# Two x tiles of a key stage: loaded together, one chain of statistics, normalised and turned two products later

## The chip, the cores and the metric

The kernel runs on one core of a Trainium2 chip. The metric is the device time of one execution in microseconds (us), the median of several runs. The core's engines each work through a queue of their own in order: TensorE (PE in the profile, its weight loads PEld) multiplies, VectorE (DVE) and ScalarE (ACT) work on tiles, GpSimd (POOL) does small arithmetic and issues some DMAs, SyncE (SP) issues most DMAs. An instruction that waits holds up all that stands behind it in the same queue.

## The reference

16 batches of 64 tokens with 512 features go through one block: cross attention with 32 heads of 128, and a linear layer with eight low-rank experts.

```
x = x + xattn(layernorm(x), ctx, mask, bias, Wq, Wk, Wv, Wo)
x = x + ffn(layernorm(x), base_W, base_b, router, A, B, expert_map)

xattn: q = xn @ Wq ; k = ctx @ Wk ; v = ctx @ Wv      # (1024 x 512) @ (512 x 4096)
       score = q k^T / sqrt(128) + bias, masked ; p = softmax(score)
       out = (p v) @ Wo
layernorm(x) = (x - mean) / sqrt(var + 1e-5)           # over the 512 features
```

All is float32. The change touches only the first layernorm, and when it is done.

## The kernel before

**Tiles and stages.** The 1024 tokens of x are eight tiles of 128 tokens. Keys and values are computed first, then queries, attention and output projection head pair by head pair, then the linear layer. A float32 product is three matmuls (`mm3`, line 256): both factors are split into a high and a low part (`split`, line 69: a cast on ACT, "gh" in the profile, and a subtraction on DVE, "gl").

**A stage.** The keys come in eight quarters of four heads, the values in stages of eight heads. Each stage is one 2 x 2 block product made with seven block products instead of eight (`winograd`, line 213). The products run in the order 1, 2, 6, 5, 7, 4, 3 (`ORDER`). In a key stage a product has two halves k (two PSUM banks), each of six matmuls. Products 1, 6, 7 and 4 add up in the same bank xb[k]; after products 1, 6 and 7 a copy of the sum so far is taken on ACT (u, u2, u3; lines 220, 227, 230), and the next product of that bank must wait for the copy. Products 5 and 3 add up in yb[k]. The results c11, c22, c21 and c12 are made by DVE and ACT into eight buffers ("ob") and stored by SP (`emit_k`, line 338).

**The order of the stages.** `stages` (line 381) lists them: quarters 0 and 1 run interleaved, then value stage, 2, 3, value stage, 4, 5, value stage, 6, value stage, 7. So quarter 5 follows quarter 4 directly. While a stage runs, the weights of the next are split.

**The x tiles.** Quarters 3 to 6 each handle two tiles of x beside their products (`keys_of`, line 366). A tile is loaded by SP (`x_tile`, line 315, xt), normalised (`norm`, line 87) and turned (`x_turn`, line 325). `norm` does, on DVE, the statistics and the aggregate (lines 92, 93) and adds 1e-5 (line 95), on POOL the power -0.5 (line 96, "rs"), on DVE the shift (line 98, "nb"), and on ACT the normalising (line 100, "xn"). `x_turn` transposes 32 x 32 blocks on DVE (line 330, "xb") and then issues 16 DMAs of 16 KB from POOL's queue, which move the blocks to their places in xT (line 333). xt, xn, xb, and later the v tiles of the attention, share four buffers (pool "v"). xT is first read after quarter 6.

**What sets the order.** The order on TensorE is written out. On DVE, ACT, POOL and SP a planner orders the instructions by the priority in which the program names them and by its own estimate of when they become ready; `tc.issue_after(ins)` adds that an instruction is queued behind `ins`. The normalising is queued behind the last copy taken so far (`copied[-1]`), the load of x behind the last store of keys (`stored[-1]`).

Of the kernel before, what the change touches and what calls it, by code (L numbers as in the profile page):

```python
# [14 lines left out]
AF = mybir.ActivationFunctionType  # L15
# [32 lines left out]
def xattn_ffn_kernel(ctx: ExitStack, tc: tile.TileContext, x, ctxT, wq, wk, wv, wo, fside, mask,  # L48
                     base_wT, base_b, arT, router_b, lora_b, expert_map, out):
    nc = tc.nc  # L50
    scale = 1.0 / math.sqrt(128.0)

    small = ctx.enter_context(tc.tile_pool(name="small", bufs=1))
    sm = ctx.enter_context(tc.tile_pool(name="sm", bufs=2))
# [11 lines left out]
    def blk(tag, name, dt=F32, shape=(P, 512)):  # L66
        return pools[tag].tile(list(shape), dt, tag=tag, name=name)
# [16 lines left out]
    nc.vector.memset(zero, 0.0)  # L84
    maskb = const.tile([P, NT, S], F32, name="maskb")

    def norm(pool, xns, xts):
        n = len(xts)
        mv = pool.tile([P, n, 2], F32, tag="mv", name="mv")
        for j, xt in enumerate(xts):  # L90
            bs = pool.tile([P, 6], F32, tag="bs", name="bs")
            nc.vector.bn_stats(bs, xt)
            nc.vector.bn_aggr(mv[:, j, :], bs)
        rs = pool.tile([P, n], F32, tag="rs", name="rs")
        nc.vector.tensor_scalar(rs, mv[:, :, 1], EPS, None, ALU.add)
        nc.gpsimd.tensor_tensor(rs, rs, nhalf[:, 0:n], ALU.pow)
        nb = pool.tile([P, n], F32, tag="nb", name="nb")
        nc.vector.scalar_tensor_tensor(nb, mv[:, :, 0], -1.0, rs, ALU.mult, ALU.mult)
        for j, (xn, xt) in enumerate(zip(xns, xts)):
            nc.scalar.activation(xn, xt, AF.Identity, bias=nb[:, j:j + 1], scale=rs[:, j:j + 1])  # L100

    def transposed(ps, xn):
        for kc in range(KC):
# [5 lines left out]
    with ExitStack() as actx:  # L109
# [103 lines left out]
        def winograd(mm, n, emit, yzbank=bank, order=ORDER):  # L213

            xb, zb, yb, u, u2, u3 = ({} for _ in range(6))

            def post(i, k):
                if i == 1:
                    u[k] = blk("sn", "u")
                    nc.scalar.copy(u[k], xb[k])  # L220
                elif i == 2:
                    c = blk("ob", "c11")
                    nc.vector.tensor_tensor(c, u[k], zb[k], ALU.add)
                    emit(0, 0, k, c)
                elif i == 6:
                    u2[k] = blk("sn", "u2")
                    copied[:] = [nc.scalar.copy(u2[k], xb[k])]
                elif i == 7:
                    u3[k] = blk("sn", "u3")
                    copied[:] = [nc.scalar.copy(u3[k], xb[k])]  # L230
                    c = blk("ob", "c22")
                    nc.vector.tensor_tensor(c, u3[k], yb[k], ALU.add)
                    emit(1, 1, k, c)
                elif i == 4:
                    c = blk("ob", "c21")
                    nc.scalar.copy(c, xb[k])
                    emit(1, 0, k, c)
                elif i == 3:
                    c = blk("ob", "c12")
                    nc.vector.tensor_tensor(c, u2[k], yb[k], ALU.add)  # L240
                    emit(0, 1, k, c)

            for i in order:
                for k in range(n):
                    if i == 1:
                        xb[k] = bank()
                    elif i == 2:
                        zb[k] = yzbank(k)
                    elif i == 5:
                        yb[k] = yzbank(k)  # L250
                    b = xb if i in (1, 6, 7, 4) else zb if i == 2 else yb
                    mm(i, k, b[k], i in (1, 2, 5))
                    post(i, k)
                yield i
# [7 lines left out]
        def mm_weights(t, g):  # L262
            def mm(i, k, o, first):
                for kc in range(2):
                    mm3(o, [a[:, kc, k * P:(k + 1) * P] for a in g[i]], [b[:, kc] for b in t[i]],
                        first and kc == 0, kc == 1)
            return mm
# [47 lines left out]
        def x_tile(t):  # L315
            nonlocal xT
            if xT is None:
                xT = ax.tile([P, KC, TOK], F32, tag="ax", name="xT")
            xt = blk("v", "xt")
            with tc.issue_after(stored[-1].ins):  # L320
                nc.sync.dma_start(out=xt, in_=x[t])
            xn = blk("v", "xn")
            return xn, xt

        def x_turn(t, xn):

            a, g = divmod(t, 4)
            dst = xT.rearrange("p k (g a b) -> p g a k b", g=4, a=2)[:, g, a]
            xb = blk("v", "xb", F32, (P, 4, KC, 32))
            nc.vector.transpose(xb, xn.rearrange("p (k j i) -> p j k i", k=KC, j=4))  # L330
            for j in range(4):
                for i in range(4):
                    nc.gpsimd.dma_start(out=dst[32 * j:32 * j + 32, :, 32 * i:32 * i + 32],  # L333
                                        in_=xb[32 * i:32 * i + 32, j])
# [3 lines left out]
        def emit_k(q):  # L338
            def emit(i, j, k, c):
                stored[:] = [nc.sync.dma_start(out=kd[4 * q + 2 * i + k][:, j * HALF:(j + 1) * HALF], in_=c)]  # L340
            return emit
# [8 lines left out]
        with tc.manual_schedule(engines={nc.tensor.engine}):  # L350
# [13 lines left out]
                    enumerate((bank, lambda k: small_bank("yz")))]  # L364

            def keys_of(q, g):
                xn = {}
                for i in winograd(mm_weights(tc_, g), 2, emit_k(q)):
                    if 3 <= q < 7:
                        t = 2 * (q - 3)  # L370
                        if i in (1, 6):
                            xn[i] = x_tile(t + (i == 6))
                        if i in (6, 7):
                            with tc.issue_after(copied[-1].ins):
                                norm(sm, *([a] for a in xn[1 if i == 6 else 6]))
                        elif i == 5:
                            x_turn(t, xn[1][0])
                        elif i == 3:
                            x_turn(t + 1, xn[6][0])

            stages = (0, "o"), (2, "k"), (3, "k"), (2, "o"), (4, "k"), (5, "k"), (4, "o"), (6, "k"), (6, "o"), (7, "k")
            ops = {}
# [17 lines left out]
            for n, (q, kind) in enumerate(stages[:-1]):  # L400
                load(n + 2)
                ops[n + 1].all()
                if kind == "k":
                    keys_of(q, ops[n])
                else:
                    for i in winograd(mm_oct(tc_, ops[n]), 4, emit_oct(q),
                                      lambda k: bank() if k < 2 else small_bank("yz")):
                        pass
                if n == 1:
                    with tc.issue_after(stored[-1].ins):  # L410
                        nc.sync.dma_start(out=m8, in_=mask)
                        nc.sync.dma_start(out=emi, in_=expert_map.partition_broadcast(P))
                        nc.sync.dma_start(out=rb, in_=router_b.partition_broadcast(P))
                    nc.vector.tensor_scalar(maskb, m8, -1.0, BIG, ALU.add, ALU.mult)
                    nc.vector.tensor_reduce(valid, m8, AX.X, ALU.max)
                    nc.vector.tensor_copy(emf, emi)
                    for e in range(E):
                        nc.vector.tensor_scalar(oneh[:, e, :], emf, float(e), 2.0, ALU.is_equal, ALU.mult)
# [91 lines left out]
            def pv_mm(i, pt, v, home="o"):  # L510
                ps = [bank() for _ in range(2)]
                for t in range(NT):
                    for a in range(2):
                        r = slice(a * S, (a + 1) * S)
                        for d in range(0, P, S):
                            c = slice(i * P + d, i * P + d + S)
                            nc.tensor.matmul(ps[a][d:d + S, t * S:(t + 1) * S], lhsT=v[t // 2][r, t % 2, c],  # L517
                                             rhs=pt[r, :, t, :], start=True, stop=True)
                res = []
                for b in range(2):  # L520
                    hl = [blk(home, f"o{c}", F32R) for c in "hl"]
                    with tc.high_priority(offset=SOON):
                        evicted[:] = split(hl[0], hl[1], ps[b])
                    res.append(hl)
                return res
# [68 lines left out]
            w, prev, added, pts, soft, ss, ns, t = None, None, None, [], [], [], 0, 0  # L594
# [12 lines left out]
            for p in range(NP):  # L607
# [3 lines left out]
                for c in steps:  # L611
                    if c == "P":
                        old, told = prev, t
                        prev, t = ([pv_mm(i, pts[i], v, "g" if p + 1 == NP else "o") for i in range(2)], w), 0
# [185 lines left out]
    xns, xbs, x2s, pas, stats = ({} for _ in range(5))  # L800
# [95 lines left out]
```

## Time and profile before

| | |
|---|---|
| three runs | 762.72, 764.22, 764.67 us; median 764.22 |
| profiled execution | span 761.7 us from first to last instruction; no other time of it is listed |
| TensorE busy | 752.5 us (99%), granted clock 0.999 |
| VectorE, ScalarE, GpSimd busy | 565.8, 412.0, 194.8 us |
| quarter 4 (first matmul of it to first matmul of quarter 5) | 159.85 to 178.89: 19.04 us |
| quarter 5 | 178.89 to 199.57: 20.68 us |
| one statistics instruction (line 92) x8 | 0.69 us |
| one power on POOL (line 96) x8 | 0.57 us |
| one normalising (line 100) x8 | 0.82 us |
| one transpose (line 330) x8 | 0.70 us |
| one turn DMA on POOL's queue (line 333) x128 | 0.55 us; landing 1.6 to 5.0 us after issue, median 2.6 |

In the lines of a time line the first number is the start in us from the span's start, the second the length; several instructions of one kind in a row are merged ("x16"); the bracket gives how long the engine was idle before, and what ended that. In a line of waits stand: who waited, for whom, us in total, times, the longest.

### The profile page before, as it was taken

The page shows a single profiled execution, that of the slowest core. Times are in us where ns is not written, and L with a number is a line of the kernel's source. Part 1 is how long each engine was busy: PE and PEld are TensorE (multiplying, and loading weights), DVE is VectorE, ACT ScalarE, POOL GpSimd, SP SyncE. Part 2 cuts the span into 40 slices and gives each one's busy share as a digit, 9 for nine tenths or more (in the row PEclk, how much of TensorE's full clock was granted, in tenths as well). Part 3 has the DMA queues.
Part 4 walks back from the last instruction along what each step waited for, and adds up shares of the span by engine and source line. Part 5 has one row for each costly group of instructions (what it writes and reads, how often), then busy time and mean ns, then how long its engine had stood idle before and what let it go on. Part 6 is the DMA issues. An engine that isn't in the chain of part 4 may idle for free.

```text
span 761.7 us, 16780 instructions
## 1 busy us (share of the span) xinstructions
PE 752.5 (99%) x6154; PEld 624.9 (82%) x6154; DVE 565.8 (74%) x1076; ACT 412.0 (54%) x1157; POOL 194.8 (26%) x271
## 2 busy tenths in 40 slices
PE   8999999999999999999999999999999999999998
PEld 6888888888788888877888888888888888888898
DVE  7986567666655776869778777787778777878975
ACT  5654444444444445667645565456645765474361
POOL 0000008108820693223220222022211232010330
PEclk9999999999999999999999999999999999999999
DMA  6685647465735446466554465436544564462011
GB/s 255 229 285 186 205 157 229 147 218 179 224 130 187 156 126 225 142 222 217 189 158 149 138 199 167 142 120 201 174 141 134 180 185 140 125 199 84 1 57 56
DMA packets 84946, 126.79 MB, mean 166 GB/s; under 512 B 11776, under 2 KB 35072, under 8 KB 84864
## 3 DMA queue, kind: packets, MB, share of 16 engines
q1 hardware_dynamic: 80624, 123.56, 49.9%
q0 software_dynamic: 4096, 2.11, 1.2%
q8 instruction: 48, 0.79, 0.5%
q14 instruction: 34, 0.28, 0.1%
q10 hardware_dynamic: 144, 0.06, 0.0%
HBM read 83.74 MB, written 35.65 MB: 157 GB/s over the span
## 4 chain that ended last, share of the span: by engine, by line
PE 91%; DVE 3%; POOL 2%; DMA 2%; issue 1%; ACT 0%; SPq 0%; DVEq 0%; ACTq 0%; POOLq 0%
PE ps L259 73%; PE yz L259 5%; PE ps L742 5%; PE ps L517 4%; PE pss L470 4%; POOL xT L333 1%; DMA cT<-in_ctxT 1%; DMA so<-in_wo 0%; DMA xT<-xb 0%; DVE bs L708 0%; DVE gl L71 0%; PE pt L104 0%; DVE s L161 0%; DVE ol L71 0%; POOL st L711 0%
## 5 line engine op out<-in xcount | busy, mean ns | idle before, releaser
L481 ACT ACTIVATE p<-p,nm 128x64 f32<-128x64 f32 x256 | 85.9, 339 | 33.3 <-DVE nm L475 31.0
L534 DVE TENSOR_TENSOR acc<-acc,ps 128x512 f32<-128x512 f32 x128 | 86.8, 681 | 21.2 <-PE ps L259 20.4
L259 PE MATMUL ps<-wh,ol 128*128 128x512 f32 x256 | 99.9, 390 | 0.8 <-DVE ol L71 0.8
L259 PE MATMUL ps<-wh,oh 128*128 128x512 f32 x256 | 100.1, 391 | 0.0
L259 PE MATMUL ps<-wl,oh 128*128 128x512 f32 x256 | 99.7, 389 | 0.0
L70 ACT CAST gh<-s 128x512 fp32r<-128x512 f32 (+1 forms) x128 | 64.4, 514 | 56.0 <-PE ps L259 45.7
L333 POOL DMA_DIRECT2D xT<-xb x128 | 69.7, 552 | 84.9 <-DVE xb L330 80.7
L71 DVE TENSOR_TENSOR gl<-s,gh 128x512 fp32r<-128x512 f32 (+1 forms) x128 | 72.0, 566 | 23.2 <-ACT gh L70 23.1
L161 POOL TENSOR_TENSOR s<-rq 128x256 f32<-128x256 f32 x32 | 25.3, 790 | 238.9 <-DMA rq<-in_wq 190.1
L71 DVE TENSOR_TENSOR ol<-ps,oh 128x512 fp32r<-128x512 f32 x64 | 39.9, 683 | 31.5 <-ACT oh L70 31.3
L70 ACT CAST gh<-raw 128x512 fp32r<-128x512 f32 x48 | 29.8, 623 | 52.8 <-PE yz L259 36.1
L259 PEld LDWEIGHTS ps<-wh,ol 128*128 128x128 f32 x256 | 48.1, 188 | 11.4 <-DVE ol L71 1.6
L259 PEld LDWEIGHTS ps<-wl,oh 128*128 128x128 f32 x256 | 48.1, 188 | 10.0
L259 PEld LDWEIGHTS ps<-wh,oh 128*128 128x128 f32 x256 | 48.0, 188 | 10.0
L71 DVE TENSOR_TENSOR gl<-raw,gh 128x512 fp32r<-128x512 f32 x48 | 35.1, 731 | 27.9 <-ACT gh L70 20.7
L461 POOL TENSOR_TENSOR bm<-bm,maskb 128x512 f32<-128x512 f32 x32 | 42.4, 1348 | 36.6 <-DMA bm<-in_fside 36.6
L481 ACT ACTIVATION_READ_ACCUMULATOR p<-p,nm 128x1 f32 x256 | 48.6, 190 | 0.0
L565 DVE TENSOR_TENSOR q<-u,ps 128x512 f32<-128x512 f32 x48 | 32.8, 683 | 20.4 <-PE ps L259 16.0
L70 ACT CAST oh<-ps 128x512 fp32r<-128x512 f32 x64 | 33.2, 590 | 11.0 <-PE ps L517 11.0
L70 ACT CAST gh<-rq 128x256 fp32r<-128x256 f32 x48 | 19.5, 406 | 36.0 <-PE ps L259 32.1
L517 PEld LDWEIGHTS ps<-pt,v 64*64 64x64 f32 x2048 | 31.9, 135 | 5.7 <-issue 5.6
L554 ACT COPY u<-ps 128x512 f32<-128x512 f32 x48 | 27.9, 581 | 15.9 <-PE ps L259 8.8
(258 smaller groups left out, 1986.2 us busy)
## 6 DMA issues: line engine op xcount, KB each, us to landing
kd<-c SPq DMA_DIRECT2D x64, 256.0 KB, 2.6
vd<-c SPq DMA_DIRECT2D x64, 256.0 KB, 2.8
kT<-kd SPq DMA_DIRECT2D x64, 256.0 KB, 3.9
v<-vd SPq DMA_DIRECT2D x64, 256.0 KB, 3.7
raw<-in_wk SPq DMA_DIRECT2D x32, 256.0 KB, 4.0
raw<-in_wv SPq DMA_DIRECT2D x32, 256.0 KB, 4.3
rq<-in_wq SPq DMA_DIRECT2D x32, 256.0 KB, 4.1
bm<-in_fside SPq DMA_DIRECT2D x32, 256.0 KB, 4.5
```

The costliest lines, as they stand in the source:

```text
L70: first = nc.scalar.copy(hi, src)
L71: return first, (lo_eng or nc.vector).tensor_tensor(lo, src, hi.bitcast(F32), ALU.subtract)
L259: nc.tensor.matmul(o, lhsT=a, rhs=b, start=first and n == 0, stop=last and n == 2, skip_group_check=True)
L333: nc.gpsimd.dma_start(out=dst[32 * j:32 * j + 32, :, 32 * i:32 * i + 32], in_=xb[32 * i:32 * i + 32, j])
L461: nc.gpsimd.tensor_tensor(bm, bm, maskb, ALU.add)
L470: nc.tensor.matmul(ps[a * S:(a + 1) * S, t, :], lhsT=qT[n // 8][:, cq], rhs=kT[m // 8][:, ck], start=True, stop=True)
L481: nc.scalar.activation(p[:, t, :], p[:, t, :], AF.Exp, bias=nm[:, t:t + 1], accum_out=sme[:, t:t + 1])
L517: nc.tensor.matmul(ps[a][d:d + S, t * S:(t + 1) * S], lhsT=v[t // 2][r, t % 2, c], rhs=pt[r, :, t, :], start=True, stop=True)
L534: return nc.vector.tensor_tensor(acc[:, t, :], acc[:, t, :], ps, ALU.add)
L554: copy = nc.scalar.copy(s[i], b["x"])
L565: add = nc.vector.tensor_tensor(self.blocks[key], s[u], b[bk], ALU.add)
L742: nc.tensor.matmul(o, lhsT=a, rhs=b, start=start, stop=stop, skip_group_check=True)
```

## The change

Before, each of the two tiles of a stage had its own load, chain of statistics, normalising and turn: the first load after product 1, the second after product 6; first tile normalised after product 6 and turned after product 5 (the one that follows 6), the second normalised after product 7 and turned after product 3.

After, both tiles are loaded after product 1. After product 6 one chain is run for both: two statistics, two aggregates, then one add, one power and one shift on tiles of 128 x 2. The first tile is normalised after product 5, the second after product 7; the first is turned after product 7, the second after product 3.

```diff
-    def norm(pool, xns, xts):
+    def normalise(pool, xns, xts):
         n = len(xts)
         mv = pool.tile([P, n, 2], F32, tag="mv", name="mv")
         for j, xt in enumerate(xts):
...
         nc.vector.scalar_tensor_tensor(nb, mv[:, :, 0], -1.0, rs, ALU.mult, ALU.mult)
-        for j, (xn, xt) in enumerate(zip(xns, xts)):
-            nc.scalar.activation(xn, xt, AF.Identity, bias=nb[:, j:j + 1], scale=rs[:, j:j + 1])
+
+        def apply(j):
+            nc.scalar.activation(xns[j], xts[j], AF.Identity, bias=nb[:, j:j + 1], scale=rs[:, j:j + 1])
+
+        return apply
...
             def keys_of(q, g):
-                xn = {}
                 for i in winograd(mm_weights(tc_, g), 2, emit_k(q)):
                     if 3 <= q < 7:
                         t = 2 * (q - 3)
-                        if i in (1, 6):
-                            xn[i] = x_tile(t + (i == 6))
-                        if i in (6, 7):
+                        if i == 1:
+                            xs = [x_tile(t + j) for j in range(2)]
+                        elif i == 6:
+                            apply = normalise(sm, *zip(*xs))
+                        elif i in (5, 7):
                             with tc.issue_after(copied[-1].ins):
-                                norm(sm, *([a] for a in xn[1 if i == 6 else 6]))
-                        elif i == 5:
-                            x_turn(t, xn[1][0])
-                        elif i == 3:
-                            x_turn(t + 1, xn[6][0])
+                                apply(int(i == 7))
+                        if i in (7, 3):
+                            x_turn(t + (i == 3), xs[int(i == 3)][0])
```

In the built program TensorE's instructions and their order are the same. On POOL each stage's queue becomes: one power, 32 turn DMAs (before: power, 16 DMAs, power, 16 DMAs; in quarter 5 power, power, 32 DMAs). On DVE the two transposes of a stage stand together, behind the second c22 of product 7. On ACT the second normalising stands ahead of the two c21 copies instead of behind them (in quarter 5 it stays where it was), and in quarter 5 the first normalising stands behind the first u3 copy and two gh instead of ahead of them.

## The prediction

> **What bounds the kernel now.** I read the page's busy shares first, then the waits of TensorE, then the time line of each engine around the one wait that lies in the changed stages.
>
> The page's first part:
>
> ```profile
> PE 752.5 (99%) x6154; PEld 624.9 (82%) x6154; DVE 565.8 (74%) x1076; ACT 412.0 (54%) x1157; POOL 194.8 (26%) x271
> ```
>
> TensorE is busy for 752.5 of 761.7 us, so an edit that leaves its instructions alone can gain only where it waits. All its long waits, in the view of waits:
>
> ```profile
> PE ps L259 <- DVE gl L71: 1.4, 2, 1.1
> PE ps L259 <- ACT u L230: 1.3, 1, 1.3
> ...
> PE ps L259 <- DVE ol L71: 0.8, 1, 0.8
> ```
>
> Only the second is in a key stage that handles x. A stage of seven products takes 19.04 us (84 matmuls at 0.2267); busy time by stretch shows which stage loses it (the second column is the length, the third PE):
>
> ```profile
> 161.00:180.00 19.00, 19.00 (x85) 15.76 (x84) 12.08 (x21) 9.37 (x16) 9.00 (x17) 1.00 0.55 181
> 180.00:200.00 20.00, 18.66 (x82) 15.12 (x81) 14.85 (x30) 10.29 (x18) 15.91 (x30) 1.00 0.49 149
> ```
>
> That is quarter 5, which follows quarter 4 with no value stage between. Its first matmul is at 178.89 and the next stage's at 199.57: 20.68 us, so 1.64 us are lost (1.34 idle, the rest slow matmuls after it). The time lines of POOL, DVE, ACT and PE show the cause:
>
> ```profile
> 170.99 8.69 POOL L333 DMA_DIRECT2D xT<-xb  x16 [34.67 <-DVE xb L330]
> 179.69 0.57 POOL L96 TENSOR_TENSOR rs<-rs,nhalf 128x1 f32<-128x1 f32 x1
> 182.59 8.69 POOL L333 DMA_DIRECT2D xT<-xb  x16 [2.33 <-DVE xb L330]
> 191.29 0.57 POOL L96 TENSOR_TENSOR rs<-rs,nhalf 128x1 f32<-128x1 f32 x1
> ```
>
> ```profile
> 174.69 0.68 DVE L232 TENSOR_TENSOR c<-u,ps 128x512 f32<-128x512 f32 x1
> ...
> 191.89 0.16 DVE L98 SCALAR_TENSOR_TENSOR nb<-mv,rs 128x1 f32<-128x1 f32 x1 [1.55 <-POOL rs L96]
> ```
>
> ```profile
> 192.14 0.81 ACT L100 ACTIVATE xn<-xt,nb,rs 128x512 f32<-128x512 f32 x1 [4.00 <-issue]
> 192.86 0.60 ACT L70 CAST gh<-s 128x512 fp32r<-128x512 f32 x1
> 193.37 0.58 ACT L230 COPY u<-ps 128x512 f32<-128x512 f32 x1
> ```
>
> ```profile
> 192.27 0.39 PE L259 MATMUL ps<-t7l,gh 128*128 128x512 f32 x1
> 193.99 0.50 PE L259 MATMUL ps<-t4h,gh 128*128 128x512 f32 x1 [1.34 <-ACT u L230]
> ```
>
> Sixteen turn DMAs hold POOL's queue for 8.69 us (0.543 each). Quarter 5's power `rs` stands behind those of quarter 4's second tile and ends at 191.86; `nb` starts 0.03 later, the normalising 0.25 after `nb`; ACT's queue holds back the copy u3 of product 7 until 193.37, and product 4, which adds onto the copied bank, starts 0.62 after the copy's start instead of at 192.49. ("issue" beside the normalising is not its reason: it starts 0.25 after `nb` at 125.00, 180.54 and 258.48 too.) Rightly read, the question is when quarter 5's `rs` comes in the changed kernel.
>
> **The change part by part.**
>
> *Fewer small instructions.* Per key stage one add (0.15), one `nb` (0.16) and one power (0.57) go: over four stages 1.2 us of DVE and 2.3 us of POOL. Cost on the path 0: PE hides all of it, DVE being idle for 26%. The second chain's waits go too (DVE 3.06 us at 124.75, 1.87 at 180.29, 1.62 at 258.24; ACT 2.63, 1.05 and 1.19). PE had no idle in those stretches, so they bring 0.
>
> *Loads together.* The second xt is issued before the stage's two c11 stores instead of after them. One issue takes SP 0.33 to 0.43, so those stores and the weight loads behind them leave about 0.4 later. In the built order the loads of quarter 5 wait only for the turns of quarter 3, long landed, and SP is not held. There are eight store buffers and the c11 stores wait for DVE anyway. 0.
>
> *One chain, quarter 3.* Now the first normalising waits for both tiles' statistics. From the first at 110.64: second statistics 111.26 (spacing 0.62), first aggregate 111.87, gl 111.97, second aggregate 112.56, s 112.68, add 113.29 (spacings 0.60, 0.10, 0.59, 0.12, 0.61), power 113.60 to 114.16, `nb` 114.19, normalising 114.44 (112.66 before). Behind it on ACT: gh 115.16 (0.72 later), u3 copy 115.67 (0.51 later; 115.23 before), product 4 possible at 116.29. It stands at 116.33 now, so 0 with 0.04 to spare; by the spread of such rows between 0 and 0.3. I take 0.
>
> *The turns two products later, quarter 4.* The first transpose moves from 169.98 to behind product 7's second c22. That stands at 174.69 and the next DVE instruction starts 0.60 later, so the transposes are at 175.29 and 175.9; the second normalising, now right after the second u3 copy (173.95), is at 174.43 and ready at 175.25. POOL starts 0.31 after the first transpose ends (170.68 to 170.99), at 176.30, and now issues 32 DMAs with nothing between: 32 x 0.543 = 17.38, to 193.68. Before, the gap of 2.33 us for the second transpose lay between the two sixteens, and the end was 191.28. So quarter 5's power is not freed: it comes 2.40 later, 193.69 to 194.26; `nb` 194.29, normalising 194.54.
>
> *The normalising later in the queue, quarter 5.* In the built order ACT now does product 7's first u3 copy and one gh ahead of the first normalising, only the second u3 copy behind it. So the first half of product 4 starts on time at 192.49 and covers 1.36, to 193.85. The second copy starts 0.72 after the normalising, 195.26; PE goes on at 195.88. Stall 195.88 - 193.85 = 2.03, with the slow restart of 0.14 it is 2.17, against 1.64: **+0.53 us**. What waits on DVE behind `nb` (two gl and s of the next stage, c22 of the second half at about 195.9) is needed at 197.24 at the earliest, when product 3 starts; its second half, which uses that c22, at 198.6. The first transpose of quarter 5 also waits for quarter 4's last turn DMA to land (issue 193.1 plus 2.2, the median landing of the second sixteen, 3.1 at most): 196.3, after that c22. No further cost.
>
> The size of this rests on the 32 issues. A row for 32 in one run does not exist. Lower bound 17.38, as the sixteens have it. POOL keeps eight in flight, so a DMA waits where the one eight before it has not landed after 8 x 0.543 = 4.34 us; the 32 issues from 194.14 to 212.90 took 18.76, with landings up to 4.9 us beside heavy weight loads. In 171 to 193 landings were at most 3.1, so I take the lower; the upper adds 1.4.
>
> [...]
>
> *Later stages.* DVE reaches the next chain's `nb` in the value stages and waits there for POOL: about 135.6 to 138 and 213 to 217 (turns of quarter 5 from 197.6 plus 18.8, plus 0.57). Behind it stand six instructions of about 0.65 before product 7's first c22 at about 223 (199.57 + 0.5 + four products of 5.44 + 1.36); 217 + 4 = 221. Hidden, with 2 us to spare; beyond that, product 4 (5.44 us) covers the c22. Quarter 6: 32 issues from about 254.6, ended near 272 to 275 (before 271.7); x's differences on POOL end near 289 instead of 285.9, first needed after 297.5. The v loads on SP, which wait for these buffers, are held to about 276 instead of 273, the stores behind them too; the next c22 need buffers at 281.7. 0.
>
> **Sum.** 0 + 0 + 0 + 0.53 + 0 = +0.5 us on the profiled execution: span 761.7 becomes 762.2. The page gives no other time of this execution; the runs are 762.72, 764.22 and 764.67, so the median lies 2.5 above the span. The same step on the median gives 764.7 us.
>
> **The rivals.**
>
> - *Slower by over 2.3 us (0.3%, about what a measurement of this kernel can tell from no change).* The run of 32 meets slow landings, so POOL stands at each group of eight. Three groups wait, so at landings of L each run costs 3 x (L - 4.34) more. At 4.9 that is 1.7, in all +2.2 (766.4); it decides from L = 4.94. For it: landings of 4.4 to 4.9 at 196 to 206. Against it: at most 3.1 in the stretch that counts.
> - *The stall goes.* The power comes before the turns, or the transposes start early enough, and the stage takes 19.04: -1.64, 762.6. Against it: the built order of POOL has power, 32 DMAs, power, and nothing before the second c22 can free the transposes.
> - *Quarter 3 becomes a second stall.* A chain 0.5 late costs 0.5 + 0.14 there: +1.2 in all, 765.4.
> - *Nothing moves.* The moved wait happens to equal the old one: 764.2.
> - *Faster by over 2.3 us.* It would need more than the one stall, such as the 1.1 and 0.8 at the start of attention, which nothing in the change reaches.
>
> **How the numbers follow.** Forecast (+0.2 to +1.0) 0.48; second stall or moderate DMA waits (+1.0 to +2.3) 0.14; slow landings or a cost I have not seen (over +2.3) 0.27; stall gone or nothing moved (-2.3 to +0.2) 0.06; faster by more 0.05. So faster 0.05, same 0.68, slower 0.27. The likeliest one's own range, with 1 us of run spread, is 763.4 to 765.8. For 8 in 10 it must reach the -1.64 case in part and the slow landings: 763.0 to 767.2.
>
> **What would show it.** Right: POOL issuing x32 from about 176.3 with the power at about 193.7; the transposes in pairs; one wait of PE for u3 of about 2 us in the middle of product 4 of quarter 5, and none elsewhere in 100 to 320. Wrong: that wait absent, landings over 4.3 us at 176 to 194, a PE wait at 116.3, or a PE wait in the value stages.

## The result and the profile after

The changed kernel takes 766.01 us (median of 12 executions, 762.95 to 771.88) against 763.59 us for the kernel before (12 executions): a ratio of 1.0032, 95% interval 1.0017 to 1.0046. A second series of 12, told below, gives 766.41 against 764.04, 1.0030 (1.0006 to 1.0054). So the change costs 2.4 us. The forecast was +0.5 (764.7 us); the time lies inside the range 763.0 to 767.2. The 2.4 us are just over the 2.3 (0.3%) from which the prediction speaks of "slower", and the interval covers both sides of that bound.

The first part of the page of the changed kernel and its longest waits of TensorE (line 262 was 259, line 233 was 230):

```profile
PE 754.2 (99%) x6154; PEld 626.1 (82%) x6154; DVE 557.9 (73%) x1068; ACT 411.4 (54%) x1157; POOL 191.8 (25%) x267
```

```profile
PE ps L262 <- ACT u L233: 2.0, 1, 2.0
PE ps L262 <- DVE gl L71: 1.1, 2, 0.6
```

The wait for u3 grew from 1.3 to 2.0. The wait of 0.8 for `ol` at the start of attention is gone. But TensorE is busy for 1.7 us more with the same 6154 matmuls: some of them ran slower. Busy time by stretch shows where; the number after the five engines is the granted clock:

```profile
180.00:200.00 20.00, 18.03 (x74) 14.48 (x73) 12.77 (x24) 9.41 (x16) 16.78 (x32) 0.92 0.51 175
```

```profile
194.00:196.00 2.00, 0.45 (x2) 0.03 (x1) 1.13 (x3) 0.92 (x2) 0.79 (x2) 1.00 0.59 209
196.00:198.00 2.00, 1.58 (x5) 1.31 (x6) 1.94 (x4) 1.55 (x3) 0.00 (x0) 0.75 0.23 90
198.00:200.00 2.00, 2.00 (x7) 1.54 (x6) 1.12 (x3) 1.10 (x2) 1.99 (x4) 0.50 0.85 304
200.00:202.00 2.00, 2.00 (x9) 1.63 (x8) 1.25 (x2) 0.00 (x0) 2.00 (x5) 0.90 0.67 215
```

The granted clock falls to a half right behind the stall of quarter 5; in the kernel before it stayed at 1.00 there. The time lines of GpSimd, VectorE, ScalarE and TensorE around the stall:

```profile
176.73 17.34 POOL L336 DMA_DIRECT2D xT<-xb  x32 [35.77 <-DVE xb L333]
194.09 0.72 POOL L96 TENSOR_TENSOR rs<-rs,nhalf 128x2 f32<-128x2 f32 x1
```

```profile
194.84 0.16 DVE L98 SCALAR_TENSOR_TENSOR nb<-mv,rs 128x2 f32<-128x2 f32 x1 [1.70 <-POOL rs L96]
```

```profile
195.08 0.81 ACT L101 ACTIVATE xn<-xt,nb,rs 128x512 f32<-128x512 f32 x1 [1.56 <-DVE nb L98]
195.80 0.56 ACT L233 COPY u<-ps 128x512 f32<-128x512 f32 x1
```

```profile
194.06 0.39 PE L262 MATMUL ps<-t4l,gh 128*128 128x512 f32 x1
196.42 0.50 PE L262 MATMUL ps<-t4h,gh 128*128 128x512 f32 x1 [1.97 <-ACT u L233]
196.76 0.42 PE L262 MATMUL ps<-t4h,gl 128*128 128x512 f32 x1
196.99 0.61 PE L262 MATMUL ps<-t4l,gh 128*128 128x512 f32 x1
197.40 0.63 PE L262 MATMUL ps<-t4h,gh 128*128 128x512 f32 x1
...
200.38 0.41 PE L262 MATMUL ps<-t3h,gl 128*128 128x512 f32 x1
200.64 0.39 PE L262 MATMUL ps<-t3l,gh 128*128 128x512 f32 x1
```

Up to 196.42 this is the chain of the prediction, 0.40 to 0.55 us later (0.35 of it from the first 25 us of the run, before any change): 32 issues in 17.34 us, the power, `nb`, the normalising, the copy, in the middle of product 4. From 196.99 to 200.38 the matmuls start 0.43 us apart instead of 0.227. That is 3.4 us at half clock, and costs about 8 x 0.2 = 1.6 us.

The stages by the first matmul of each, in the two profiled executions:

| | before | after | difference |
|---|---|---|---|
| first product 5 of the run | 23.85 | 24.20 | +0.35 |
| from there to quarter 5 (holds quarter 3) | 155.04 | 155.13 | +0.09 |
| quarter 5 (19.04 without a loss) | 20.68 | 22.92 | +2.24 |
| from there to the first output product (350.24 before) | 150.67 | 149.38 | -1.29 |
| from there to the last matmul | 407.91 | 407.65 | -0.26 |

So this execution shows only +1.1 us (span 762.9; device time 764.7, which is 1.3 below the median of its series) although quarter 5 alone costs 2.24: the stretch up to the first output product gave 1.29 back.

### The profile page after: what moved, and what is told of

It is laid out like the page before. It is cut to its first block, busy times and chain, and to the rows that moved or that the text cites. A ratio compares the mean times of both kernels' runs of the same rounds, so it can differ in the third digit from the quotient of the medians.

```text
span 762.9 us, 16787 instructions
## 1 busy us (share of the span) xinstructions
PE 754.2 (99%) x6154; PEld 626.1 (82%) x6154; DVE 557.9 (73%) x1068; ACT 411.4 (54%) x1157; POOL 191.8 (25%) x267
## 4 chain that ended last, share of the span: by engine, by line
PE 91%; POOL 3%; DVE 2%; DMA 2%; issue 1%; ACT 1%; SPq 0%; DVEq 0%; ACTq 0%; POOLq 0%
PE ps L262 72%; PE yz L262 5%; PE ps L744 5%; PE ps L519 4%; PE pss L472 4%; POOL xT L336 2%; DMA rq<-in_wq 1%; DMA cT<-in_ctxT 1%; DVE bs L710 0%; PE pt L107 0%; DVE s L164 0%; DVE q L567 0%; SPq L300 0%; DVE gl L71 0%; POOL st L713 0%
## 5 line engine op out<-in xcount | busy, mean ns | idle before, releaser
L262 PEld LDWEIGHTS ps<-wh,ol 128*128 128x128 f32 x256 | 48.1, 188 | 10.5 <-DVE ol L71 0.7
L71 DVE TENSOR_TENSOR gl<-raw,gh 128x512 fp32r<-128x512 f32 x48 | 33.0, 691 | 30.8 <-ACT gh L70 22.9
L472 PEld LDWEIGHTS pss<-kT,q 128*64 128x64 f32 x1024 | 31.3, 138 | 6.3 <-issue 5.6
```

The source lines that it names most:

```text
L71: return first, (lo_eng or nc.vector).tensor_tensor(lo, src, hi.bitcast(F32), ALU.subtract)
L262: nc.tensor.matmul(o, lhsT=a, rhs=b, start=first and n == 0, stop=last and n == 2, skip_group_check=True)
L472: nc.tensor.matmul(ps[a * S:(a + 1) * S, t, :], lhsT=qT[n // 8][:, cq], rhs=kT[m // 8][:, ck], start=True, stop=True)
```

## The experiments

**Theory A:** the idle time of TensorE, grown to 2 us, makes the clock fall, and this is the time over the forecast. **Theory B:** the fall, or the time, belongs to something else in the change. The listed mean granted clock of an execution tells whether the clock fell: 3.4 us at half clock make 1 - 1.7/763 = 0.998. Of the first 12 executions of the changed kernel nine show 0.998 or less, and three show 1.0. "Lost" below is quarter 5's length less 19.04, in the profiled execution. The ratios are those of the comparison of all executions, not quotients of the two medians.

**The stall alone, longer, in the kernel before.** One, two or five further powers with exponent 1 stand behind quarter 5's first power; no other part of the change is there. In short:

```
+        for _ in range(extra):                  # 1, 2 or 5, for the first tile of quarter 5 only
+            nc.gpsimd.tensor_tensor(rs, rs, one[:, 0:n], ALU.pow)
```

> The kernel before, with one further small power (to the exponent 1) on GpSimd behind quarter 5's first power; nothing else moves on any engine. It makes the one stall of the kernel before longer by one power, 0.57 us: TensorE idle 1.34 + 0.57 = 1.91, about the 1.97 of the changed kernel, without any of the change's loads, chains or turns. Theory A (the length of the idle time decides: the granted TensorE clock falls to half for about 3.4 us after an idle time of about 2 us, and does not after 1.34): granted clock 0.998 in most executions, matmuls spaced 0.43 instead of 0.227 us for some 3.4 us after the stall, 763.6 + 0.57 + 1.6 = 765.8 us; an execution in which the clock does not fall 764.2. Theory B (the fall of the clock, or the time over the forecast, belongs to something else in the change): clock 1.0 in all, 763.6 + 0.57 = 764.2 us.

> The kernel before with two further small powers at the same place: TensorE idle 1.34 + 1.14 = 2.48 us. Theory A: the clock falls at least as often as with one, 763.6 + 1.14 + 1.6 = 766.3 us. Theory B: clock 1.0, 763.6 + 1.14 = 764.7 us.

> The kernel before with five further small powers behind quarter 5's first power: TensorE idle 1.34 + 5 x 0.61 = 4.4 us. Theory A (the fall of the clock comes from the length of the idle time): the clock falls in every execution, none at 1.0, 764.0 + 3.05 + 1.6 = 768.7 us. Theory B (falls are unrelated to the stall): about a third of the executions below 1.0, as for the kernel before, 764.0 + 3.05 = 767.0 us.

TensorE at the end of the wait, with one, two and five powers more:

```profile
195.99 0.50 PE L262 MATMUL ps<-t4h,gh 128*128 128x512 f32 x1 [1.96 <-ACT u L233]
196.33 0.39 PE L262 MATMUL ps<-t4h,gl 128*128 128x512 f32 x1
```

```profile
195.10 0.50 PE L262 MATMUL ps<-t4h,gh 128*128 128x512 f32 x1 [2.58 <-ACT u L233]
...
196.33 0.63 PE L262 MATMUL ps<-t4h,gl 128*128 128x512 f32 x1
```

```profile
196.00 0.80 PE L262 MATMUL ps<-t4h,gh 128*128 128x512 f32 x1 [3.95 <-ACT u L233]
...
200.86 0.58 PE L262 MATMUL ps<-t4l,gh 128*128 128x512 f32 x1
201.27 0.39 PE L262 MATMUL ps<-t3h,gh 128*128 128x512 f32 x1
```

| further powers | idle | lost | median, kernel before beside it | ratio, 95% | at 0.998 or less |
|---|---|---|---|---|---|
| 1 | 1.96 | 2.25 | 765.76, 763.98 | 1.0018 (1.0003 to 1.0032) | 5 of 12 |
| 2 | 2.58 | 4.48 | 766.97, 763.98 | 1.0040 (1.0024 to 1.0057) | 7 of 12 |
| 5 | 3.95 | 6.70 | 769.16, 764.04 | 1.0056 (1.0033 to 1.0079) | 9 of 9 |

With one power the profiled execution kept its clock behind 1.96 us of idle time; with two and with five it fell. With five the half clock lasted two stretches of 3.41 us (194.42 to 201.24; 1.58 us of the idle time lay in the first of them), which is why 6.70 us were lost. Theory A's medians (765.8, 766.3, 768.7) are met within 0.7, B's (764.2, 764.7, 767.0) are missed by 1.6 to 2.3. The medians alone do not prove A, and with one power the nearness is partly luck. In its profile the clock fell at 8 us, not behind the stall, and executions at 1.0 are late as well: with one power six average 764.95, with two five average 766.21, where the kernel before at 1.0 on that chip averages 763.49 and the stall grew by 0.62 and 1.24. About 0.8 and 1.5 us of that have no cause on record. The kernel before, over the four chips, is at 0.998 or less in 31 of 113 executions (27%); with one, two and five powers it is 42%, 58% and 100%. "In most executions" was too much for the 1.96, and 5 of 12 cannot be told from 27%.

**The same stall, filled.** The changed kernel again, and the changed kernel with TensorE kept busy in the wait (the edit in short, 14 for the constant `FILL`):

> The changed kernel itself once more, beside the kernel before on one chip. If the time over the forecast is the fall of the clock behind quarter 5's stall: the stall of 1.97 us stands in every execution, executions with a granted clock of 1.0 take 764.2 us (0.5 over 763.6) and those at 0.998 about 766; median 766. If the first twelve executions were only unlucky: median 764.2, clock mostly 1.0.

```
+                    if q == 5 and i == 4 and k == 1:        # ahead of the second half of product 4
+                        w = small_bank("fill")
+                        for _ in range(14):
+                            nc.tensor.matmul(w[:, 0:256], lhsT=zero[:, 0:P], rhs=zero, start=True, stop=True)
                     mm(i, k, o, first)
```

> The changed kernel with fourteen matmuls on a tile of zeros (128x256, result never read) on TensorE between the two halves of product 4 of quarter 5, where it otherwise stands idle for 1.97 us. At full clock they take 14 x 0.11 = 1.5 us, so they end before the wait does and put off nothing; the wait on u3 and what follows stay. Theory A (the clock falls because TensorE is idle): idle time left about 0.5 us, no fall behind it, clock 1.0 about as often as in the kernel before (two thirds of the executions), 766.2 - 1.7 = 764.5 us. Theory B (the fall has another cause in that place, such as the burst of work or the transfers after the stall): the fall stays in three of four executions, 766.2 us.

The repeat has the stall and the fall once more:

```profile
196.27 0.50 PE L262 MATMUL ps<-t4h,gh 128*128 128x512 f32 x1 [2.25 <-ACT u L233]
...
197.64 0.63 PE L262 MATMUL ps<-t4h,gl 128*128 128x512 f32 x1
```

766.41 against 764.04, nine of 12 at 0.998 or less, lost 4.15. With the filling:

```profile
193.97 1.70 PE L377 MATMUL fill<-zero 128*128 128x256 bf16 x14
196.29 0.50 PE L263 MATMUL ps<-t4h,gh 128*128 128x512 f32 x1 [0.62 <-ACT u L234]
196.63 0.40 PE L263 MATMUL ps<-t4h,gl 128*128 128x512 f32 x1
196.86 0.39 PE L263 MATMUL ps<-t4l,gh 128*128 128x512 f32 x1
```

Product 4 goes on at the same place (196.29), but at full clock: lost 2.44 instead of 3.88 and 4.15. The median is 764.88 against 764.38, ratio 1.0009 (0.9990 to 1.0027), with three of 12 at 0.998 or less, like the kernel before. Theory A's 764.5 is met, theory B's 766.2 is not. This shows the cause of the fall behind this stall: the wait is as long as before (2.32 us from 193.97 to 196.29), only the idleness is gone, and with it the fall (18 of 24 executions of the changed kernel at 0.998 or less, 3 of 12 with the filling). What is left, +0.5 of the medians, agrees with the forecast's number, but its interval (-0.8 to +2.1 us) also holds none.

**The stall taken away.** The last four (kernel before) or eight (changed kernel) turn DMAs of quarter 4's second tile go to SyncE's queue.

```
-                    nc.gpsimd.dma_start(out=dst[...
+                    eng = nc.sync if t == 3 and 4 * j + i >= 12 else nc.gpsimd      # 8 in the changed kernel
+                    eng.dma_start(out=dst[...
```

> The kernel before, with the last four of the sixteen turn DMAs of quarter 4's second tile issued by SyncE instead of GpSimd. GpSimd reaches quarter 5's power 4 x 0.543 = 2.17 us earlier, at about 189.1, the normalising is at about 190.0, behind a cast of weights, and the stall of 1.64 us goes; the four issues hold SyncE for some 1.5 us. Both theories: no wait of TensorE for u3 in quarter 5, clock 1.0, and 763.6 - 1.64 = 762.0 us if nothing downstream takes it back; 763.6 if the waits at the start of attention (1.08 and 0.81 in the profile of before) are set by something that does not move with TensorE and so grow by the same.

> The changed kernel, with the last eight of the sixteen turn DMAs of quarter 4's second tile issued by SyncE. GpSimd reaches quarter 5's power 8 x 0.543 = 4.34 us earlier, at about 189.7, and the stall of 1.97 us goes. Theory A: the fall of the clock goes with it: clock 1.0 in all executions, 766.0 - 2.1 - 1.7 = 762.2 us. Theory B: the stall goes and the rest stays, 766.0 - 2.1 = 763.9 us.

GpSimd in the kernel before with four turns on SyncE:

```profile
182.76 6.52 POOL L334 DMA_DIRECT2D xT<-xb  x12 [2.33 <-DVE xb L330]
189.29 0.56 POOL L96 TENSOR_TENSOR rs<-rs,nhalf 128x1 f32<-128x1 f32 x1
```

The power ends 2.0 us earlier, the wait for u3 is gone in both, lost 0.00 and 0.32. So the turn DMAs ahead of the power are the stall's cause. The medians are 763.96 and 764.33 against 763.98: 1.0005 (0.9991 to 1.0018) and 1.0012 (0.9994 to 1.0030). The first lies at the expected upper end, 763.6: the 1.64 us gained did not reach the end. The second misses A's 762.2 by 2.1: six of its 12 executions are at 0.998 or less, and its profile has no stall in quarter 5, so these falls must have come from elsewhere; the executions in which they fell were not profiled. The six series without that stall (here and below) are at 0.998 or less in 21 of 72 executions (29%), between 1 and 6 of 12, so one series of 12 says little about the share.

**The parts of the change.**

```
loads alone        xn[1], xn[6] = x_tile(t), x_tile(t + 1)      # after product 1; the rest as before
loads and chain    both loads after 1, one chain after 6; normalised after 6 and 7, turned after 5 and 3
later turns        a load and a chain for each tile as before; normalised after 5 and 7, turned after 7 and 3
```

> Only the second x tile's load brought forward to the first's; a chain of statistics and a power for each tile, normalising and turns where the kernel before has them. It tells whether the gain of the loads and the chain in quarter 5 needs the one chain. If the early load alone does it: the second transpose of quarter 4 comes at about 178 instead of 182.3, GpSimd is through its turn DMAs at about 188.4 and no wait for u3 stands in quarter 5, 1.5 us less at the end of that stage. If the one chain is needed: the stall of 1.34 us stays and the time is that of the kernel before.

> The loads together and the one chain of the change, with the first tile's normalising and turn at their old places (after products 6 and 5). The second transpose comes some 2 us after the first, so GpSimd has all 32 turn DMAs of quarter 4 out by about 171.0 + 17.4 = 188.4, quarter 5's power ends at about 189.1 and the stall there goes. If the later turns are what costs in the change: no wait for u3 in quarter 5, 763.6 - 1.64 = 762.0 us, or up to 764.0 where the start of attention takes it back as in the run with four turns on SyncE (763.96 against 763.98), clock mostly 1.0. If the loads or the chain cost: 765 us or more, with a wait in quarter 3 (product 4 at about 116.5) or in a value stage.

> The loads together and the one chain alone, once more, since its profile was 1.6 us below that of the kernel before at the end and its median was not. If the 1.6 us that it gains in quarter 5 reach the end: 762.4 against 764.0 over both runs; if they are taken back: within 0.5 of the kernel before.

> The loads together and the one chain alone, a third time, to say whether it is faster than the kernel before: 0.8 to 1.6 us below it if the gain in quarter 5 reaches the end, within 0.5 us if it does not.

> The other half: loads, statistics and powers for each tile by itself as before, only the normalising and the turn of the first tile two products later. The 32 turn DMAs of quarter 4 run without a gap from about 176.3 to 193.7, as in the changed kernel, and quarter 5's power stands behind them. If the later turns are what costs: a wait for u3 of about 2 us in quarter 5 and 766.0 us, clock 0.998 in more than half of the executions. If not: 764.0 us.

GpSimd with the loads alone, then with the later turns alone and its stall on TensorE:

```profile
170.43 17.32 POOL L333 DMA_DIRECT2D xT<-xb  x32 [33.59 <-DVE xb L330]
187.77 1.09 POOL L96 TENSOR_TENSOR rs<-rs,nhalf 128x1 f32<-128x1 f32 x2
```

```profile
175.47 17.32 POOL L336 DMA_DIRECT2D xT<-xb  x32 [4.53 <-DVE xb L333]
192.81 1.09 POOL L96 TENSOR_TENSOR rs<-rs,nhalf 128x1 f32<-128x1 f32 x2
```

```profile
194.94 0.50 PE L262 MATMUL ps<-t4h,gh 128*128 128x512 f32 x1 [1.75 <-ACT u L233]
195.28 0.39 PE L262 MATMUL ps<-t4h,gl 128*128 128x512 f32 x1
```

| | lost | median, kernel before beside it | ratio, 95% | at 0.998 or less |
|---|---|---|---|---|
| loads alone | 0.00 | 763.61, 763.79 | 0.9997 (0.9981 to 1.0012) | 4 of 12 |
| loads and chain | 0.00 | 764.35, 764.04 | 0.9995 (0.9972 to 1.0018) | 3 of 12 |
| the same again | 0.00 | 762.64, 764.38 | 0.9983 (0.9966 to 1.0001) | 1 of 12 |
| a third time | 0.00 | 764.41, 763.79 | 1.0012 (0.9998 to 1.0027) | 6 of 12 |
| later turns | 2.05 | 765.16, 764.04 | 1.0009 (0.9990 to 1.0029) | 4 of 12 |

The early load by itself closes the gap between quarter 4's two runs of sixteen DMAs; the 32 start at 170.43 and the stall vanishes. Putting the turns two products later moves the same 32 to 175.47, and the stall comes back, 0.41 more lost than before. By itself that falls short of the expected 2 us: the first of its two powers of one column ends after 0.57 us, so the normalising does not wait for 0.72 us of power. That is 0.15 of the 0.22 us between its wait (1.75) and the changed kernel's (1.97). In its profile the clock held there; at 765.16, with an interval of -0.8 to +2.2 us, its series does not say whether the later turns alone cost anything. Both profiles of the changed kernel, where the two halves are together, have a wait of about 2 us (1.97 and 2.25).

Without a stall quarter 5 is 1.64 us shorter in every one of these profiles, yet no series is clearly faster than the kernel before. The three series of loads and chain give -0.4, -1.3 and +0.9 us by their ratios. From quarter 5 to the first output product the six profiles without a stall need 149.9 to 151.9 us (before 150.67), and from there to the end 408.1 to 413.5 (before 407.91). So what follows spreads by more than the gain. Whether something there takes the gain back as a rule is open. No version here is shown to beat the kernel before; loads and chain without the later turns, at 763.8 us over its three medians, stands below the changed kernel.

## Why the prediction was right, and where it fell short

- *Fewer small instructions*, *Loads together*: 0 was taken, and no wait of TensorE appears beside them. Between 100 and 320 us the wait for u3 is its only one. But the early load by itself frees the power (the run with the loads alone); it is the later turns that undo this, and the prediction did not see the two apart.
- *One chain, quarter 3*: bounds 0 to 0.3; measured +0.09, and +0.27 in the repeat. Within the bounds, but the spare 0.04 was used up. The power of two columns takes 0.71 us there, not the 0.56 taken over from one column, which is the likely reason.
- *The turns two products later, quarter 4*: transposes in a pair, 32 issues in a run from 176.73, 17.34 us long where 17.38 was taken (lower bound; the upper was 18.76). In the repeat the same run took 17.6. The power did stand behind the turns: each held GpSimd's queue for 0.542 us (17.34 / 32), and the power started at 194.09, when the last had been issued (194.07).
- *The normalising later in the queue, quarter 5*: first half of product 4 on time, second copy at 195.80, TensorE idle from 194.29 (the start at 194.06 plus 0.227) to 196.42: 2.13 where 2.03 was worked out. The 0.10 more is mostly the longer power (0.15).
- **The term that failed** is "with the slow restart of 0.14 it is 2.17". The 0.14 was the cost behind an idle time of 1.50 us by the same count (192.49 to 193.99; the profile prints 1.34) and was carried over to one of 2.03. In the profile it measured 3.88 - 2.13 = 1.75 us, because the clock fell to a half for 3.41 us; with the idle time filled 2.44 - 2.32 = 0.12 is left of it.
- *Slow landings*: not so; the 32 issues did not stand, and they landed within 1.7 to 3.8 us. That such an issue waits for the landing of the DMA eight before it is read from quarter 5 of the kernel before. The turns issued at 196.34 and 197.41 landed 4.4 and 4.8 us later; the issues eight behind them stood until 0.3 us after that:

```profile
201.06 1.09 POOL L333 DMA_DIRECT2D xT<-xb  x2 [0.40 <-DMA xT<-xb]
202.45 3.40 POOL L333 DMA_DIRECT2D xT<-xb  x6 [0.30 <-DMA xT<-xb]
```

- *The stall goes*: that is what the loads alone do, and the later turns undo. *Quarter 3 becomes a second stall* and *Nothing moves*: not so. *Faster by over 2.3*: it was said that nothing in the change reaches the two waits at the start of attention; they did move, from 1.08 and 0.81 to 0.41 and none; the stretch is 1.29 us shorter in the profile of the changed kernel. Nothing of the change is needed for it. In the kernel before with one, two and five powers, where only the stall is longer, the stretch is 1.46, 1.41 and 1.05 us shorter too: a TensorE that comes later finds less to wait for there. One profile each is not proof, and the kernel with the filling, whose quarter 5 is 0.8 us longer, needed 0.39 us more.
- *Later stages*: quarter 5's turns ran from 198.01 to 216.75 and the next power came at 216.77, where at most 217 was expected, and no wait of TensorE stands in a value stage.

Split by clock, the sum can be read more directly. The six executions of the changed kernel at 1.0 average 764.17 us; the 66 of the kernel before at 1.0, over four chips, average 763.73: +0.44, where +0.53 was forecast, though six executions carry this only to about half a microsecond. The 18 at 0.998 or less average 767.37, and this is more than one fall of 1.75 us explains. Three of them are at 0.993 and average 771.24; a mean of 0.993 over 763 us means some 10.7 us at half clock by estimate, three stretches instead of one. The other 15 average 766.59, 2.4 above those at 1.0; the 0.7 us over one fall have no cause on record.

The mechanism up to the stall and the sign were right. That the time lies inside the range is in part luck: the upper end of 767.2 was there for slow landings of the turn DMAs, which did not occur, and a fall of the clock, which no term names, filled the room. The chance of "slower" (0.27) was given to slow landings or a cost not seen, and it was the latter.

## What to carry to other kernels

Here an idle gap of TensorE was not priced by its length alone. Behind 1.97 us in the changed kernel the clock fell to a half for 3.41 us, which added 1.75 us; behind 1.96 us in the kernel with one further power it held. The gap grew from 1.3 to 2.0 us, and in the profile in which the clock fell quarter 5 grew by 2.24 us, more than three times as much. The mean clock differed from execution to execution of one kernel (18 of 24 of the changed kernel at 0.998 or less), so this gap had a chance and not a fixed price. Look at the granted clock and at the spacing of the matmuls behind every wait near that length; shorten the gap, or fill it with matmuls whose result nobody reads (here quarter 5 then lost 2.44 us instead of 3.88 and 4.15). And ask of each group of DMAs issued by an engine that also computes what small instruction stands behind it: here 32 of them at 0.542 us stood ahead of one power.

## What the hardware showed that was not expected

- *How long an idle time the clock bore.* By the length of the gap the profiles cannot be sorted: the clock held behind 1.34, 1.75 and 1.96 us, and fell behind 1.97, 2.25, 2.58 and 3.95, and also behind 1.82 and 2.03 at another place (next point). The place in time sorts them. Within each of the 14 profiles the granted clock changes only at moments that lie whole multiples of 3.41 us apart, and where these moments lie differs from execution to execution (6.11 and 760.46 us in that of the kernel before; 5.85, 197.00, 200.41 and 763.61 in that of the changed kernel). Cut into such stretches, the 1.96 us of the kernel with one further power lie 1.71 in one stretch and the rest in the next, and the clock held. The 1.82 us at 497 in the second profile of loads and chain lie in one stretch, and it fell (the columns are length, PE busy, the four other engines, granted clock):

```profile
192.34:195.75 3.41, 1.70 (x8) 1.08 (x6) 1.10 (x5) 1.61 (x3) 1.97 (x4) 1.00 0.13 38
195.75:199.17 3.42, 3.18 (x14) 2.64 (x15) 3.38 (x7) 2.85 (x6) 3.03 (x6) 1.00 0.25 73
```

```profile
494.63:498.04 3.41, 1.59 (x76) 1.35 (x67) 1.29 (x2) 1.27 (x3) 3.41 (x5) 1.00 0.59 173
498.04:501.45 3.41, 3.41 (x10) 2.67 (x9) 2.49 (x4) 2.21 (x5) 0.53 (x1) 0.50 0.57 184
```

Past the first 12 us every stretch at full clock with 1.82 us or more of idle time was followed by one at half clock, and none with 1.71 or less was. The 1.75 us of the later turns alone were split into 0.93 and 0.82, the 1.34 us of the kernel before into 1.19 and 0.15. If this sorting holds, the same gap costs 1.6 us in one execution and nothing in the next: an estimate from 14 profiles, for no run here moved a gap on purpose to try it.

- *Waits with no releaser in the profile.* In eight of the fourteen profiles TensorE stands still for 0.73 to 1.06 us before one and the same matmul of the attention (at 372 to 375 us), and in two of them also for 1.82 and 2.03 us at about 497, where the clock fell as well. What holds TensorE up there is open. From the kernel with the later turns alone:

```profile
497.59 0.34 PE L522 MATMUL ps<-pt,v 64*64 64x64 f32 x8 [2.03 <-issue]
497.87 0.78 PE L262 MATMUL ps<-t5h,gh 128*128 128x512 f32 x1
498.45 0.63 PE L262 MATMUL ps<-t5h,gl 128*128 128x512 f32 x1
498.88 0.63 PE L262 MATMUL ps<-t5l,gh 128*128 128x512 f32 x1
```

- *The clock also fell at the start.* With one further power the granted clock was 0.50 from 8.0 to 11.4 us, and the run was 1.4 us late at the first product 5; in the third profile of loads and chain it was 0.50 from 7.1 to 10.5 us, and 1.2 us late. The stretches ahead of these two falls had only 1.18 and 1.17 us of idle time, so the sorting above does not hold there. These falls, and those at 497, are places from which the quarter or so of executions at a lower clock in kernels without a long stall can come.
- *A power on GpSimd* mostly takes 0.54 to 0.57 us for 128x1 and 0.71 to 0.73 for 128x2 (once each 0.98, 1.00 and 1.06 in three profiles).
